# A graph network's edge loop: groups of edges taken in pairs, in place of one by one

## The chip, the core and the metric

The kernel runs on one core of one Trainium2 chip. The metric is the device time of one execution in microseconds (us). The core has five engines that run beside each other, each with its own queue, in order: PE (TensorE, matmuls and transposes; its weight loads are shown as PEld), DVE (VectorE), ACT (ScalarE), POOL (GpSimd) and SP (SyncE, here only a DMA queue). ACT and POOL issue DMAs too.

## The reference, cut to what matters

A graph network over 12500 nodes of 64 values and 200000 edges, sorted by destination:

```
nodes = x[edges]                               # rows of source and destination, side by side: 128 values
gates = ssp(edge_state @ We1 + be1) @ We2 + be2
gates = gates * (1 - sigmoid(5 * (distance - 3.5)))
h = ssp(nodes @ Wn1 + bn1) @ Wn2 + bn2
message_sum = zeros_like(x).at[destination].add(h * gates)
new = x + ssp(message_sum @ Ws1 + bs1) @ Ws2 + bs2
out = layernorm(x + new)
```

`ssp` is softplus less log 2. So each edge needs two small networks (one over its own 64 values, one over its two nodes), a product, and an addition into its destination's row; each node then needs one more small network and a layernorm.

## The kernel before, in words

**Tiling.** The edges are cut into 391 groups of 512, each of four slots of 128 edges. All is float32, but for biases, which come as three bfloat16 pieces. A step of the main loop (line 697) does the first layer of group i+1 and the second layer of group i.

**Where the node rows come from.** The source rows of a slot are gathered from memory by an indirect DMA that POOL issues (`gather`, line 248, the DMA on line 258), 14 groups ahead (`AHEAD`), into one of 19 buffers `xg`. Such a buffer is free when the scatter of the group 19 before has read it. Two other ways take some slots off POOL. 26 slots are fetched row by row by DMAs on ACT's queue, nine rows in each step (`read_rows` and `fetch`, lines 265 and 276: three after the copy of the transposes, three after the exp, three after the log; the row numbers come from memory into registers, line 272). 23 slots are copied by DVE, eight columns in a step, out of a transposed x that lies in SBUF (`columns`, line 319). So 1514 gathers remain of 1564 slots. The destinations of a sorted group fall into two windows of 42 rows; their first layer is worked out ahead for all nodes into a table in DRAM, and `load` (line 300) brings a group's windows of that table (`wns`) and its edge values (`eT`) by SP.

**A step, engine by engine.** The code writes out the order by hand (`manual_schedule`), and each engine follows it:

- PE: `transposes` of group i+1 (four), `layer1_bias`, `layer2_bias` of group i, `scatter` of group i-2 (messages times one-hots, into windows), `layer1_edge`, `layer1_node`, and `layer2` of group i (two matmuls for the gates, four for the nodes, which need the softplus of group i).
- ACT: `xcopy` (the transposes out of PSUM), `exps` over 768 columns, `logs`, and between them the nine row DMAs.
- DVE: `window` (scattered sums added to `sums` in SBUF), `hcut` (second layer of the nodes times the distance factor), `message` (times the gates), `softplus` (an SBUF and a PSUM operand), `onehot` of group i+3, and the column copies.

PSUM holds two `z` tiles of two banks, two `gh` tiles and two `tx` tiles. In the second layer the edges lie on the partitions, so gates, nodes and messages come out with one edge per partition.

**Nodes.** 25 blocks of up to 512 nodes are finished as soon as no later group can add to them; their parts (`node_block`, line 455) are spread over the steps that follow, with PE's parts after `layer2`. The last twelve steps scatter one group back in place of two (`CLOSE`). The two last groups and the last block are written out after the loop (from line 749).

**Ahead of the loop** stands the preparation: table rows by PE, ACT and DVE, and the first 14 groups' gathers.

## Time and profile before

| | us |
|---|---|
| median of 3 runs | 1936.83 (1936.46 to 1937.05) |
| the profiled execution's own time | 1936.46 |
| its span, first to last instruction | 1934.7 |
| first transposes of the loop | at 79.5 |
| first gather issued, last gather issued | at 3.3, at 1906.3 |
| PE, DVE, ACT, POOL busy | 1776.3, 1299.2, 965.0, 1441.5 |

In the profile's lines a line number is that of the kernel's code, `out<-in` names tiles, `x` and a number is a count. ACTq and SPq are the queues of ACT and SP issuing DMAs, which do not count as busy time. In a wait, the engine and line on the left stood idle until the one on the right was done; the numbers are the total in us, how often, and the longest. "issue" is time in which an engine waited for nothing that the profile shows. PE's ends are modelled: matmuls overlap, so the starts tell more than the lengths.

### The profile page before, as it was taken

What the parts mean: (1) busy time and instruction counts of PE and PEld (TensorE: products, weight loads), DVE (VectorE), ACT (ScalarE), POOL (GpSimd) and SP (SyncE); (2) the same over time, 40 slices, a digit from 0 to 9 for tenths busy, and PEclk for the clock granted to TensorE, in tenths of its full rate; (3) what the DMA queues carried; (4) which work ended last, traced back from release to release, by engine and by line L of the source; (5) the groups of instructions that cost most, each with busy time, mean ns of one, the idle gap of its engine ahead of it and who ended that gap; (6) DMA issues with size and microseconds to landing.
All of it is one profiled execution on the core that took longest, in us unless ns stands there. A gap on an engine that the chain in (4) does not pass through costs nothing.

```text
span 1934.7 us, 48239 instructions
## 1 busy us (share of the span) xinstructions
PE 1776.3 (92%) x11419; PEld 1458.4 (75%) x11419; DVE 1299.2 (67%) x5743; ACT 965.0 (50%) x1318; POOL 1441.5 (75%) x1518
## 2 busy tenths in 40 slices
PE   4899999999999989899999998999999999999997
PEld 3787877877787777777777777777787777777775
DVE  4467776777776666666667666676677667677765
ACT  1355555555555545544445554554455555555553
POOL 7777777777777777777777777777777777777773
PEclk9999999999999999999999999999899999999998
DMA  9632222223232222222232222222232222233221
GB/s 245 230 80 66 71 73 65 72 66 73 66 74 67 64 70 64 69 65 70 64 69 67 68 69 67 70 69 67 64 75 68 69 70 70 69 73 72 70 66 25
DMA packets 146498, 147.57 MB, mean 76 GB/s; under 512 B 46735, under 2 KB 93371, under 8 KB 146082
## 3 DMA queue, kind: packets, MB, share of 16 engines
q1 hardware_dynamic: 89578, 92.27, 16.5%
q0 software_dynamic: 48448, 49.71, 13.4%
q10 hardware_dynamic: 8184, 2.44, 0.6%
q8 instruction: 97, 1.59, 0.3%
q14 instruction: 191, 1.56, 0.3%
HBM read 134.61 MB, written 9.63 MB: 75 GB/s over the span
## 4 chain that ended last, share of the span: by engine, by line
PE 43%; ACTq 19%; issue 10%; DVE 8%; ACT 8%; DMA 7%; DVEq 2%; POOL 2%; SPq 1%; POOLq 0%
ACTq L284 16%; PE z L380 9%; PE gh L419 6%; PE z L436 6%; PE tx L356 5%; PE z L373 4%; ACT xT L363 4%; PE gh L414 4%; DMA xg<-in_x,src_i 3%; ACTq L272 3%; ACT u L394 2%; POOL xg L258 2%; DVE h L428 2%; PE gh L407 2%; PE z L368 2%
## 5 line engine op out<-in xcount | busy, mean ns | idle before, releaser
L258 POOL DMA_INDIRECT xg<-in_x,src_i x1514 | 1441.3, 952 | 465.5 <-issue 332.9
L394 ACT ACTIVATE u<-z 128x768 f32<-128x768 f32 x392 | 317.4, 810 | 693.3 <-PE z L380 591.8
L453 DVE TENSOR_TENSOR sums<-sums,z 64x42 f32 x778 | 153.0, 197 | 498.2 <-ACT u L394 457.5
L380 PE MATMUL z<-xT,wns 106*128 106x256 f32 x1564 | 422.7, 393 | 10.5 <-ACT xT L363 10.1
L397 ACT ACTIVATE u<-u,one 128x768 f32<-128x768 f32 x392 | 366.1, 934 | 67.3 <-ACT u L394 62.4
L419 PE MATMUL gh<-consts,s 128*128 128x64 f32 x3128 | 397.6, 270 | 0.0
L419 PEld LDWEIGHTS gh<-consts,s 128*128 128x128 f32 x3128 | 387.0, 195 | 0.1
L402 DVE SCALAR_TENSOR_TENSOR s<-u,z 128x768 f32<-128x768 f32 x392 | 369.0, 941 | 12.2 <-ACT u L397 10.4
L380 PEld LDWEIGHTS z<-xT,wns 106*128 106x128 f32 x1564 | 297.2, 195 | 76.8 <-ACT xT L363 31.6
L356 PE MATMUL tx<-consts,xg 128*106 128x128 f32 x1538 | 239.5, 276 | 94.2 <-DVE h L428 22.0
L436 PEld LDWEIGHTS z<-xg,msg 128*128 128x128 f32 x1556 | 205.2, 192 | 125.2 <-issue 122.6
L363 ACT COPY xT<-tx 106x512 f32<-106x512 f32 x391 | 228.2, 584 | 128.1 <-PE tx L356 119.2
L332 DVE COPY column<-xh 128x1 f32 x2944 | 266.3, 147 | 25.6 <-issue 24.6
L436 PE MATMUL z<-xg,msg 128*128 128x84 f32 x1556 | 265.4, 293 | 0.4
L414 PEld LDWEIGHTS gh<-consts,s 128*128 128x128 f32 x1564 | 240.5, 196 | 29.7 <-DVE s L402 8.8
L356 PEld LDWEIGHTS tx<-consts,xg 128*106 128x106 f32 x1538 | 172.1, 140 | 111.6 <-issue 57.2
L373 PE MATMUL z<-eT,consts 128*128 128x256 f32 x782 | 254.0, 407 | 0.0
L414 PE MATMUL gh<-consts,s 128*128 128x128 f32 x1564 | 245.8, 280 | 3.9 <-DVE s L402 3.6
L428 DVE TENSOR_TENSOR h<-gh,cut 128x256 f32<-128x256 f32 x391 | 165.9, 424 | 27.9 <-PE gh L419 15.1
L432 DVE TENSOR_TENSOR msg<-gh,h 128x256 f32<-128x256 f32 x391 | 165.9, 424 | 13.4
L407 PE MATMUL gh<-row,ones 3*128 3x512 bf16 x391 | 147.3, 377 | 0.0
L342 DVE TENSOR_TENSOR xg<-consts,rel 128x168 f32<-128x168 f32 x391 | 128.3, 328 | 0.0
(102 smaller groups left out, 725.8 us busy)
## 6 DMA issues: line engine op xcount, KB each, us to landing
xr<-in_x ACTq DMA_DIRECT2D x3328, 0.2 KB
eT<-in_eT SPq DMA_DIRECT2D x195, 256.0 KB
xg<-in_x,src_i POOLq DMA_INDIRECT x1514
wns<-table SPq DMA_DIRECT2D x782, 21.0 KB
table<-tb SPq DMA_DIRECT2D x14, 448.0 KB
sums<-in_xT SPq DMA_DIRECT2D x7, 455.0 KB
y<-in_x SPq DMA_DIRECT2D x24, 128.0 KB
out<-y SPq DMA_DIRECT2D x24, 128.0 KB
```

What stands on the lines that cost most here:

```text
L258: note(("gather", g), nc.gpsimd.indirect_dma_start(out=xg[:, k, :D], out_offset=None, in_=x, in_offset=bass.IndirectOffsetOnAxis(ap=src_i[ ...
L284: ins = queues[queue].dma_start(row_tiles[n, "in"][r : r + 1, :D].bitcast(U8), x_bytes[:, bass.ds(row_at[queue].pop(0), 4 * D)])
L356: ins = nc.tensor.transpose(tx[:, k, :], xgs[g][:, k, :DW], ident)
L363: note(("xcopy", g), nc.scalar.copy(xT, xTs[g]))
L373: nc.tensor.matmul(zs[g][:, 0, :HE], we1.rearrange("a h d -> a (h d)"), eTs[g], start=False, stop=True, skip_group_check=True)
L380: nc.tensor.matmul(zn, wns[:, g % REST, h, :], xTs[g][:, h], start=True, stop=not chosen, skip_group_check=True)
L394: nc.scalar.activation(us[g][:, part], z_of(g)[:, part], AF.Exp)
L397: nc.scalar.activation(us[g][:, part], us[g][:, part], AF.Ln, bias=one)
L402: nc.vector.scalar_tensor_tensor(ss[g].rearrange("p i t e -> p (i t e)")[:, part], us[g][:, part], BIG, z_of(g)[:, part], OP.min, OP.max)
L414: nc.tensor.matmul(v[:, 0, t], ss[g][:, 0, t, :], we2, start=False, stop=False, skip_group_check=True)
L419: nc.tensor.matmul(ghs[g][:, 1, 2 * t + h, :], ss[g][:, 1 + h, t, :], wn2, start=False, stop=h == 1 and t == 1, skip_group_check=True)
L436: ins = nc.tensor.matmul(sc, msgs[g][:, 2 * t : 2 * t + 2, :].rearrange("p h f -> p (h f)"), xgs[g][:, 2 * t : 2 * t + 2, D:DW], start=t = ...
```

## The change

Groups 0 to 371 are taken in 186 pairs. A pair p (groups 2p and 2p+1) is worked like this:

- **First layer, in two halves.** `pair_edge` does bias and edge matmul for both groups at once (512 columns), `pair_node` the nodes of the first group into the same z tile; `pair_exps`, `pair_logs` and `pair_softplus` take these 1024 columns in one instruction each, then the second group's 512 columns in another.
- **Second layer, transposed.** `pair_gates` (one matmul over 512 columns) and `pair_hidden` (two over 512 columns, for the two halves of the output's partitions) leave the values on the partitions and the edges along the columns. So the biases become one value per partition: ACT adds the gates' (`pair_bias`, a new instruction over 512 columns), DVE adds the nodes' and multiplies by the gates in one instruction (`pair_products`). The bias matmul of the second layer goes. PE transposes the product back (`pair_turn`, four), and DVE multiplies by the distance factor (`pair_weigh`), which gives the messages. `hcut` and `message` go.
- **Scatter** of the pair before stands between `pair_hidden` and `pair_turn`; its windows are added after the second exp.
- **Other work.** Per pair: 18 row DMAs on ACT in six threes, sixteen column copies on DVE in two blocks of eight, two groups' loads and gathers. Column slots are used two groups later after their copies. The table rows are loaded two groups further ahead (`LOADS` 7, nine buffers), and wait for the scatter of 15 groups before in place of 9. The signs that choose between the two halves of the transposed x come in 23 small transfers, one per slot, in place of one transfer and one scaling ahead of the loop; each slot has a mask instruction for it.
- The remaining groups (from the 373rd on) go one by one as before, scattering one group back, with one-hots one group earlier and one buffer for the exps in place of two.

The number of gathers, of row DMAs and of column copies stays. The diff, cut to its core:

```diff
-LOADS = 5
+LOADS = 7
-CLOSE = 12
+PAIRS = 186
...
-        if (g - 3 - COLUMNS_FROM + 1) * COLUMNS >= (len(slots) + 1) * P:
+        if (g - 5 - COLUMNS_FROM + 1) * COLUMNS >= (len(slots) + 1) * P:
...
-        old = ("scatter", g - LOADS - 4)
+        old = ("scatter", g - LOADS - 8)
...
+            side_tiles[slot] = pool.tile([P, P], I32, name="side", bufs=1)
+            nc.sync.dma_start(side_tiles[slot], a["sides"][n : n + P].partition_broadcast(P))
...
+            mask = pool.tile([P, P], F32, name="mask", bufs=1)
+            nc.vector.tensor_scalar(mask, side_tiles[slot], sign, border, OP.mult, OP.is_ge)
...
+            nc.vector.tensor_mul(chosen_columns[slot], mask, column_tiles[slot])
...
-            us[g] = work.tile([P, 3 * HE], F32, name="u")
+            us[g] = work.tile([P, 4 * HE], F32, name="u0", bufs=1)[:, : 3 * HE]
...
+    def pair_edge(p):
+        z1s[p] = z_tile()
+        nc.tensor.matmul(z1s[p][:, 0], be3.rearrange("q h d -> q (h d)"), ones3, start=True, stop=False,
+                         skip_group_check=True)
+        nc.tensor.matmul(z1s[p][:, 0], we1.rearrange("a h d -> a (h d)"), eT2s[p], start=False, stop=True,
+                         skip_group_check=True)
+
+    def pair_node(p, j):
+        z = (z2s if j else z1s)[p]
+        for h in range(2):
+            node_half(2 * p + j, h, z[:, 1, h * HE : (h + 1) * HE])
+
+    def pair_z(p, j):
+        return z2s[p][:, 1] if j else z1s[p].rearrange("p b e -> p (b e)")
+
+    def pair_exps(p, j):
+        u2s[p, j] = work.tile([P, (2 if j else 4) * HE], F32, name=f"u{j}", bufs=1)
+        nc.scalar.activation(u2s[p, j], pair_z(p, j), AF.Exp)
+
+    def pair_logs(p, j):
+        nc.scalar.activation(u2s[p, j], u2s[p, j], AF.Ln, bias=one)
+
+    def pair_softplus(p, j):
+        if j == 0:
+            s2s[p] = work.tile([P, 6 * HE], F32, name="s2")
+        nc.vector.scalar_tensor_tensor(s2s[p][:, slice(4 * HE, 6 * HE) if j else slice(0, 4 * HE)], u2s[p, j], BIG,
+                                       pair_z(p, j), OP.min, OP.max)
+
+    def pair_gates(p):
+        gates2[p] = gh_tile()
+        nc.tensor.matmul(gates2[p], we2.rearrange("a h d -> a (h d)"), s2s[p][:, :NB], start=True, stop=True,
+                         skip_group_check=True)
+
+    def pair_hidden(p):
+        hidden2[p] = gh_tile()
+        nodes = s2s[p][:, NB:].rearrange("p (j h e) -> p h j e", j=2, h=2)
+        for h in range(2):
+            nc.tensor.matmul(hidden2[p][h * D : (h + 1) * D].rearrange("p (j e) -> p j e", j=2), wn2, nodes[:, h],
+                             start=True, stop=True, skip_group_check=True)
+
+    def pair_bias(p):
+        turned2[p] = work.tile([P, NB], F32, name="mT")
+        nc.scalar.activation(turned2[p], gates2[p], AF.Identity, bias=sides2[:, 0:1])
+
+    def pair_products(p):
+        nc.vector.scalar_tensor_tensor(turned2[p], hidden2[p], sides2[:, 1:2], turned2[p], OP.add, OP.mult)
+
+    def pair_turn(p):
+        for t in range(K):
+            part = slice(t * P, (t + 1) * P)
+            nc.tensor.transpose(hidden2[p][:, part], turned2[p][:, part], ident)
+
+    def pair_weigh(p):
+        msg2s[p] = work.tile([P, 2, K, D], F32, name="msg2")
+        nc.vector.tensor_mul(msg2s[p].rearrange("p j k d -> p (j k) d"), hidden2[p].rearrange("p (k d) -> p k d", d=D),
+                             cut[:, 2 * p : 2 * p + 2, :].rearrange("p j k -> p (j k)").to_broadcast([P, 2 * K, D]))
+
+    def pair_scatter(p, sc):
+        for j in range(2):
+            msgs[2 * p + j] = msg2s[p][:, j]
+            scatter(2 * p + j, sc[:, j * 2 * W : (j + 1) * 2 * W])
+
+    def pair_windows(p):
+        _, at = nc.values_load_multi_w_load_instructions(
+            base_i[0:1, 4 * p : 4 * p + 4], engines=[DVE], min_val=0, max_val=N - 1,
+            skip_runtime_bounds_check_because="they were clamped to these bounds")
+        for j in range(2):
+            window_at[2 * p + j] = at[2 * j : 2 * j + 2]
+            window(2 * p + j)
...
-                    nc.vector.tensor_scalar(sides, sides_i, sign, None, OP.mult)
...
+            for p in range(-1, PAIRS):
+                i, m, single = 2 * p, 2 * p + 2, p == PAIRS - 1
+                now = [parts.pop(i, []), parts.pop(i + 1, [])]
+                for j in range(2):
+                    at(load, i + LOADS + 1 + j)
+                if 0 <= p < XH_PARTS:
+                    part = slice(half_n * p // XH_PARTS, half_n * (p + 1) // XH_PARTS)
+                    nc.sync.dma_start(xh[:, part], a["xh"][:, part])
+                for j in range(2):
+                    if p >= 0:
+                        at(gather, i + AHEAD + j)
+                transposes(m, ("load", m), ("gather", m), ("onehot", m))
+                xcopy(m)
+                read_rows(i, 1, ROWS[1])
+                fetch(i, 1, 3)
+                if single:
+                    layer1_bias(m)
+                    layer1_edge(m)
+                else:
+                    pair_edge(p + 1)
+                if p >= 0:
+                    pair_gates(p)
+                    pair_bias(p)
+                if p >= 1:
+                    pair_weigh(p - 1)
+                fetch(i, 1, 3)
+                if single:
+                    layer1_node(m)
+                    exps(m)
+                else:
+                    pair_node(p + 1, 0)
+                    pair_exps(p + 1, 0)
+                fetch(i, 1, 3)
+                transposes(m + 1, ("load", m + 1), ("gather", m + 1), ("onehot", m + 1))
+                for j in range(2):
+                    at(onehot, i + 4 + j)
+                for j in range(2):
+                    columns(i + j, finish)
+                if p >= 0:
+                    pair_hidden(p)
+                for part in now[0] + now[1]:
+                    if part.tensor:
+                        part.tensor(tx_tile())
+                if p >= 0:
+                    pair_products(p)
+                if single:
+                    logs(m)
+                    xcopy(m + 1)
+                    layer1_bias(m + 1)
+                    layer1_edge(m + 1)
+                else:
+                    pair_logs(p + 1, 0)
+                    xcopy(m + 1)
+                    z2s[p + 1] = z_tile()
+                read_rows(i + 1, 1, ROWS[1])
+                fetch(i + 1, 1, 3)
+                if p >= 1:
+                    pair_scatter(p - 1, zs[m + 1][:, 1, HE:] if single else z2s[p + 1][:, 0])
+                if p >= 0:
+                    pair_turn(p)
+                if single:
+                    layer1_node(m + 1)
+                    exps(m + 1)
+                    fetch(i + 1, 1, 3)
+                    logs(m + 1)
+                    softplus(m)
+                else:
+                    pair_node(p + 1, 1)
+                    pair_exps(p + 1, 1)
+                    fetch(i + 1, 1, 3)
+                    pair_logs(p + 1, 1)
+                    pair_softplus(p + 1, 0)
+                fetch(i + 1, 1, 3)
+                for part in now[0]:
+                    part.others()
+                if p >= 1:
+                    pair_windows(p - 1)
+                if single:
+                    softplus(m + 1)
+                else:
+                    pair_softplus(p + 1, 1)
+                for part in now[1]:
+                    part.others()
+                plan(i)
+            for i in range(2 * PAIRS + 1, last - 1):
...
+                if i == open_at + 1:
+                    pair_weigh(PAIRS - 1)
+                    layer2_bias(open_at)
+                    layer2(open_at)
+                    hcut(open_at)
+                    message(open_at)
+                layer1_bias(i + 1)
+                if i == open_at + 1:
+                    pair_scatter(PAIRS - 1, zs[i + 1][:, 1, HE:])
+                    layer1_edge(i + 1)
+                    layer1_node(i + 1)
+                    layer2_bias(i)
+                    scatter(i - 1, zs[i + 1][:, 1, HE + 4 * W : HE + 6 * W])
+                else:
+                    layer2_bias(i)
+                    scatter(i - 1, zs[i + 1][:, 1, HE : HE + 2 * W])
+                    layer1_edge(i + 1)
+                    layer1_node(i + 1)
+                exps(i + 1)
...
```

## The prediction

> **What bounds the kernel now.** I read the page's shares first: PE is busy for 92% of the span, POOL for 75%. Busy time alone would name PE, so the second view is POOL's own: the gather's line and its waits.
>
> ```profile
> PE 1776.3 (92%) x11419; PEld 1458.4 (75%) x11419; DVE 1299.2 (67%) x5743; ACT 965.0 (50%) x1318; POOL 1441.5 (75%) x1518
> ```
>
> ```profile
> L258 POOL DMA_INDIRECT xg<-in_x,src_i x1514: 941/947/2392, 3.3 to 1906.3; - x190
> ```
>
> ```profile
> POOL xg L258 <- issue: 332.9, 1091, 0.3
> POOL xg L258 <- DMA xg<-in_x,src_i: 40.3, 129, 1.0
> ```
>
> 1514 gathers have a median of 0.947 us (the three numbers are shortest, median, longest), and before each POOL stands 0.3 us whatever is named; only two such gaps are longer, the longest 1.0. So gathers follow each other every 1.25 us without a break: from 3.3 to 1906.30 + 0.95 = 1907.25 us that is 1903.9 us, 1.257 each, and 4.87 us per group. POOL is never held up; the 75% are 0.947/1.25.
>
> Third, the stages: busy time by stretch, and the waits of PE in two stretches.
>
> ```profile
> 100.00:300.00 200.00, 197.89 (x1333) 161.08 (x1331) 138.99 (x628) 109.65 (x142) 151.34 (x160) 1.00 0.29 71
> 600.00:800.00 200.00, 181.80 (x1179) 148.96 (x1178) 133.30 (x604) 99.31 (x134) 151.19 (x161) 0.98 0.28 66
> ```
>
> ```profile
> PE z L380 <- ACT xT L363: 3.8, 10, 0.6
> ...
> PE tx L356 <- DVE h L428: 21.0, 29, 1.3
> PE tx L356 <- DVE msg L432: 18.3, 15, 1.6
> PE tx L356 <- DVE sums L453: 13.5, 24, 1.3
> PE tx L356 <- DMA xg<-in_x,src_i: 11.5, 12, 1.5
> ```
>
> Columns of the first: stretch, length, busy time (records) of PE, PEld, DVE, ACT, POOL, then clock and DMA. POOL is the same in both; PE is full early and not later. A step has 28 matmul records (4+1+1+4+2+4+4+8), so 1333 are 47.6 steps: 4.20 us each. In the waits, the first line is from 100 to 560 us, where no transposes wait at all; the others are from 600 to 1900, where the first transposes of a step wait. Those DVE lines name work long done; the gather's landing is what is left. So the gathers start 71 us ahead (group 0's fourth ends at 7.21 + 0.95 = 8.2, its transposes begin at 79.5), PE gains 0.67 us a group, has caught up near 600, and then POOL sets the pace. At the end group 390 is transposed 2.3 us after the last gather, and 25.1 us of tail follow.
>
> ```profile
> 1906.30 0.95 POOL L258 DMA_INDIRECT xg<-in_x,src_i  x1 [0.30 <-issue]
> ...
> 1909.58 0.60 PE L356 MATMUL tx<-consts,xg 128*106 128x128 f32 x4
> ```
>
> Fourth, one early step on ACT, where nothing waits for gathers:
>
> ```profile
> 300.96 0.94 ACT L397 ACTIVATE u<-u,one 128x768 f32<-128x768 f32 x1 [0.16 <-ACT u L394]
> 301.04 0.85 ACTq L284 DMA_DIRECT2D xr<-in_x  x3
> 301.93 0.59 ACT L363 COPY xT<-tx 106x512 f32<-106x512 f32 x1
> 302.89 1.09 ACTq L284 DMA_DIRECT2D xr<-in_x  x3
> 304.08 0.81 ACT L394 ACTIVATE u<-z 128x768 f32<-128x768 f32 x1 [1.56 <-PE z L380]
> 304.16 0.85 ACTq L284 DMA_DIRECT2D xr<-in_x  x3
> 305.05 0.94 ACT L397 ACTIVATE u<-u,one 128x768 f32<-128x768 f32 x1 [0.16 <-ACT u L394]
> ```
>
> ACT's queue, 50% busy by its share, is full here: exp to log 0.97, log to copy 0.97, copy to exp 2.15 (a register load of 0.8 and three row loads), 4.09 in all. PE's starts in the same step also add up to 4.09: transposes 0.54, two biases 0.12 and 0.30, scatter 0.51, edges 0.47, nodes 0.87, second layer 0.44 and 0.84. Both would carry 4.09; POOL gives 4.87.
>
> **The change part by part.** The sum is made against the profiled execution, 1936.46 us: 3.3 before the first gather, 1903.9 of gathers, 27.5 after them, 1.8 around the span. It is the lowest of the three runs, 0.4 below their median.
>
> *POOL.* Row slots (26) and column slots (23) keep their number, so 1514 gathers remain: 0. They need the xg buffer of 19 groups before, freed by that group's scatter. Laid out with the rows above, the pairs' transposes begin at 79.5, 85.6 (no second layer comes before) and 94.7 (9.1 later), and scatter(0), 7 us on in that pair, ends near 101.7; gather 19 comes at 103.9. Cover 2.2 us, growing by over half a us per pair: 0, at worst a few us once if the start slips.
>
> *PE per pair.* 8 transposes 1.08, bias over 512 columns 0.30 (the 512-wide bf16 row), edges and gates 512 wide twice the 256-wide 0.47 at most, 0.90 each, nodes 1.74, hidden two 512-wide 1.80 (0.9 if its two halves, on different output partitions, run together; no row shows it, I take 1.80), scatter 1.02, four transposes back 0.54: 8.3, against 8.2 for two steps.
>
> *DVE per pair.* Softplus 512 and 768 wide take 0.68 and 0.94, so 1024 takes 1.20; second softplus 0.68; products 0.68; weigh 0.69 (0.42 at 256, and 0.26 per 256); windows 0.80; one-hots 0.66; columns 2 x 0.63 and 0.6 for the second register load: 6.6, against 6.3. Waits it adds: products stand behind hidden and, in DVE's order, behind the copies (these end about 8.5 us after the pair's first log, hidden at 8.8), and the turn on PE, with the second nodes behind it, waits for products; windows wait for the second exp, and second softplus, weigh, one-hots and copies queue behind them, with about 0.7 us to spare before hidden ends. If that cover goes, the excess lands on the second nodes.
>
> *ACT per pair*, along its queue, where it is tightest. Log over 1024: 0.51, 0.72, 0.93 at 256, 512, 768, so 1.15, less the 0.09 by which an independent instruction starts before its neighbour's end (a 0.51 log at 1913.18, the next exp at 1913.60); copy 0.59; nodes and the way to the next exp 1.25 (302.52 to 303.70, and 0.07); exp to log with three loads 0.97; log to copy 0.97; copy, register load and three loads 2.09; the new bias with three loads 1.03 (its 0.58 lies under them); exp over 1024 1.05 and 0.04. Sum 9.05. The second register load and three loads lie under log and copy. So a pair takes 9.05 where nothing disturbs it, against 8.18 for two steps: slower free, but below POOL's 2 x 4.87 = 9.74. Node blocks add 0.8 of ACT per block (log pair 0.45, root 0.33), 24 blocks, 0.1 per pair; their PE and DVE parts, mostly covered, as much; slow-clock stretches 0.1 (the late clock is 0.97, 3% of PE's 8.3 is 0.25, and its slack of 0.8 takes over half). I take 9.35, between 9.05 and 9.6; the upper end carries twice the 0.25 by which before's free steps exceed 4.09 on average (from 100 to 560 us, 106 second-layer biases are recorded, 4.34 each).
>
> *Does it still catch up?* 94.7 + 184 pairs + 18 groups x 4.09 must be at most 1909.6, less 3 for the change-over (step 373 carries a second layer more, 1.3, and waits for its message, 1.7): the limit is 9.44 per pair. At 9.35 PE reaches the gathers before the end.
>
> *SP's queue, single steps, tail.* Loads for two groups are issued per pair, for three pairs later (28 us), and wait for a scatter two pairs back; 23 small side transfers stand among them. Waits for table rows, 8.4 us in all after 600 us, lie in the gathers' waits anyway: 0, and if the loads came late, such waits again. The single steps have one buffer for exps in place of two: softplus ends at 303.02, the next exp comes at 304.08, so 0. The last 330 instructions of PE and 420 of DVE are the same in both, so the tail stays; its clock is 0.51 from 1917 on, and a shift of that costs or saves 1 to 2 us.
>
> *Start.* The scaling of sides goes. A gather beside it (45.16, 1.84 instead of 0.95) loses 0.9: -0.9. All stretched gathers before 90 us together lose 7; they bound the gain.
>
> Sum: 1936.46 - 0.9 = about 1936.
>
> **Rules weighed.** Row: a gather beside eight column copies (303.12, copies from 303.18) takes 0.97, and the median of all is 6 ns over the shortest. I price sixteen copies in one block at 0, and if each of 186 blocks cost 0.02 more, at 4 us. The Trainium skill, SBUF — State Buffer, section SBUF: two separate sides, says that an fp32 copy within SBUF locks GpSimd out of descriptor writing; by it up to 16 x 0.147 = 2.4 us per pair would be lost, 437 us in all. The scaling of sides agrees with it, one-column copies do not.
>
> Row: PE waited 1.46 us before 1007.46, and from 1009.0 to 1012.4 the clock was 0.55. The change gathers PE's waits into one of about 1.3 us per pair, which may call such stretches oftener; one costs up to 1.7 us, and the slack above 9.05 makes it good in three pairs, so I price it at 0.1. The Trainium skill, TensorE: Matmul & The Clock Gate, section Why this matters for your kernels, asks only for gaps under about 3 us; by it the price is 0. The row contradicts that.
>
> **Rivals.**
> 1. *Slower: the pair's own pace sets the end.* Place: ACT's queue from log to log, through copy and second nodes. For: 9.35 has only 0.1 to spare, and 9.6 lies in its bounds. Against: double register loads, the main excess there, are covered in the pair. From 9.44 on it decides, 18.4 us per 0.1: at 9.6, 1966; at 9.8, 2003. Chance 0.39.
> 2. *Faster: fewer stretched gathers.* At most -7 and -2 of tail: 1928 to 1933. For: traffic and a 1.77 us DVE instruction leave the start. Against: the other casts there stay. 0.07.
> 3. *The change doesn't tell* (forecast): gathers set the end. 0.54.
>
> **How the numbers follow.** 0.2% (3.9 us) is about what a measurement here can tell from no change: 1932.9 to 1940.7. The forecast's own range is 1933 to 1940. Two in ten are left out: 0.06 below 1932, 0.14 of the slower case above 1966.
>
> **What would show it.** Right: gathers every 1.25 us to about 1907, PE waiting at the transposes of a pair's second group late in the run, ACT's chain 9.1 long early on. Wrong: POOL gaps over 0.3 us late in the run (buffers not freed), or the transposes never waiting for gathers, or copies stretching gathers.

## The result, and the profile after

| | before | after |
|---|---|---|
| median | 1936.64 us (1936.19 to 1937.05, 4 runs) | 1945.54 us (1944.63 to 1951.97, 4 runs) |
| the profiled execution, its span | 1936.46, 1934.7 | 1944.63, 1942.8 |
| first transposes of the loop | 79.5 | 82.0 |
| last gather done | 1907.2 | 1912.3 |
| last group's transposes behind it | 2.3 | 5.2 |

The ratio is 1.0053, with a 95% interval of 1.0031 to 1.0075: slower by some 9 us. I had forecast 1936.0. Of the 8.1 us between the two spans, 5.1 are there when the last gather is done, and 3.0 come behind it (from its end to the end of the span it is 30.5 us instead of 27.5).

From the page of the changed kernel, PE's share and the gathers, and from POOL's waits the line of the ordinary gap and the line that is new (total us, how often, longest):

```profile
PE 1669.8 (86%) x7887; PEld 1022.7 (53%) x7887; DVE 1306.3 (67%) x5396; ACT 1069.6 (55%) x1504; POOL 1442.5 (74%) x1518
...
L257 POOL DMA_INDIRECT xg<-in_x,src_i x1514 | 1442.3, 953 | 469.6 <-issue 320.7
```

```profile
POOL xg L257 <- issue: 320.7, 1051, 0.3
...
POOL xg L257 <- DVE mT L506: 6.2, 4, 5.1
```

PE has 107 us less to do, and it bought nothing. POOL has the same 1514 gathers at the same 0.95 us, but one wait of 5.1 us among them that the kernel before did not have.

The stages by busy time (PE, PEld, DVE, ACT, POOL, then clock, DMA share, GB/s):

```profile
100.00:300.00 200.00, 177.75 (x818) 104.61 (x816) 128.34 (x525) 114.12 (x154) 147.49 (x156) 0.98 0.31 79
600.00:800.00 200.00, 177.30 (x811) 104.48 (x811) 137.17 (x587) 113.44 (x156) 151.46 (x160) 0.98 0.28 68
1500.00:1700.00 200.00, 168.09 (x801) 98.35 (x800) 138.86 (x592) 114.12 (x164) 151.49 (x160) 1.00 0.28 69
```

POOL is level at 151 from 600 us on, as before; in the first stretch it has 156 gathers where the kernel before had 160. PE is no longer full early (178 of 200, before 198).

PE's waits from 100 to 560 us (two lines, all that the view has), then from 1400 to 1830 us:

```profile
PE z L381 <- ACT xT L366: 36.9, 48, 1.4
PE gh L511 <- DVE mT L506: 14.3, 21, 2.6
...
PE tx L359 <- DMA xg<-in_x,src_i: 26.4, 22, 1.8
PE tx L359 <- DMA wns<-table: 12.0, 13, 1.9
```

Early, PE waits within the pair: for ACT's copy of the second transposes, and for DVE's products. Late, the transposes wait for the gathers (13 of the waits are put down to the table rows, `wns`, which land about then). So the order of things is the forecast's: the pair's own chain sets the pace first, the gathers later. The lag of a group's transposes behind its last gather says when: 57.7 us at group 20, 3.1 at group 260 (transposes at 1285.2), and then about 2 (1.9 in the median, never under 1.5) up to group 374. It ends otherwise than before:

```profile
1911.38 0.95 POOL L257 DMA_INDIRECT xg<-in_x,src_i  x1 [0.30 <-issue]
...
1917.56 0.60 PE L359 MATMUL tx<-consts,xg 128*106 128x128 f32 x4
```

### Where the first 5 us come from

The start, from the timelines (start, length, then what ended the idle time before it). L651 in the kernel before and L727 in the changed one are the matmuls of the table ahead of the loop, L356 and L359 the transposes; L745 are the new matmuls that make the biases of the transposed second layer, L440 is the scatter. First PE in the kernel before, up to the transposes of group 2; then the changed kernel: PE ahead of the loop, PE in its first steps, and POOL, where the first line is the 77th gather in the kernel before (L258) and the last the 77th in the changed one:

```profile
35.08 12.32 PE L651 MATMUL z<-consts,sums 65*128 65x128 f32 x56 [10.98 <-DVE tb L654]
48.32 24.26 PE L651 MATMUL z<-consts,sums 65*128 65x128 f32 x112 [0.93 <-DVE tb L654]
79.50 1.07 PE L356 MATMUL tx<-consts,xg 128*106 128x128 f32 x4 [6.92 <-DMA wns<-table]
...
90.19 1.06 PE L356 MATMUL tx<-consts,xg 128*106 128x128 f32 x4
```

```profile
33.82 6.34 PE L727 MATMUL z<-consts,sums 65*128 65x128 f32 x28 [9.15 <-DVE tb L730]
44.38 0.21 PE L745 MATMUL gh<-ones,rows 3*128 3x1 bf16 x2 [4.21 <-DVE rows L742]
44.52 30.71 PE L727 MATMUL z<-consts,sums 65*128 65x128 f32 x140
```

```profile
82.00 1.07 PE L359 MATMUL tx<-consts,xg 128*106 128x128 f32 x4 [6.78 <-DMA wns<-table]
...
90.08 2.07 PE L381 MATMUL z<-xT,wns 106*128 106x256 f32 x4 [1.91 <-ACT xT L366]
91.95 1.06 PE L359 MATMUL tx<-consts,xg 128*106 128x128 f32 x4
...
101.32 0.60 PE L359 MATMUL tx<-consts,xg 128*106 128x128 f32 x4
...
106.60 1.12 PE L440 MATMUL z<-xg,msg 128*128 128x84 f32 x8
```

```profile
103.87 0.94 POOL L258 DMA_INDIRECT xg<-in_x,src_i  x1 [0.30 <-issue]
...
101.45 0.95 POOL L257 DMA_INDIRECT xg<-in_x,src_i  x1 [0.31 <-issue]
107.55 0.95 POOL L257 DMA_INDIRECT xg<-in_x,src_i  x1 [5.15 <-DVE mT L506]
```

Two tiny matmuls (0.21 us) stand in PE's order in the middle of the table's matmuls and wait 4.21 us for a DVE copy; 140 table matmuls queue behind them. In the kernel before PE's table work ran from 35.08 to 72.58 us with one gap of 0.93; here it ends at 75.2, and the loop starts 2.5 us later. Then the first pair is slow: PE's matmuls take up to twice as long (four transposes 1.06 us, 0.60 later), and PE waits 1.91 us for the copy. Half the clock is the likely reason. The clock's view does not show it here (1.00 from 80 to 95 us), but in late_fewer, one of the runs below, the same transposes (at 88.14 there) take 1.06 too, and the clock is 0.71 from 85 to 90 us and 0.61 from 90 to 95. The kernel before starts as slowly. So the first scatter comes at 106.60, and the gather that needs its buffer, the 77th (76 in the expectations, which count from 0), starts at 107.55, where it could have started at 102.7. (The profile puts this wait down to DVE's products, L506, which end at about the same time. The buffer is the one that group 0's scatter reads, the first four of the eight matmuls at 106.60.) These 4.8 us are never won back, since the gathers run at their own pace from there to the end: 1804.8 us from that one's start to the last one's end, where the kernel before took 1803.4. The sum for POOL is 4.8 of waiting and 1.4 of slightly slower gathers, less 1.2 that it is ahead before the wait: 5.1 with the unrounded numbers.

### Where the last 3 us come from

The passage from pairs to single steps, PE's timeline:

```profile
1837.82 0.60 PE L359 MATMUL tx<-consts,xg 128*106 128x128 f32 x4
...
1841.44 1.12 PE L440 MATMUL z<-xg,msg 128*128 128x84 f32 x8 [1.01 <-DVE msg L515]
...
1845.98 0.38 PE L359 MATMUL tx<-consts,xg 128*106 128x128 f32 x2
...
1848.35 0.68 PE L440 MATMUL z<-xg,msg 128*128 128x84 f32 x4 [1.34 <-DVE msg L436]
...
1852.82 0.74 PE L579 MATMUL tx<-consts,l_s 128*128 128x128 f32 x4 [0.97 <-DVE l_s L571]
1853.39 0.60 PE L359 MATMUL tx<-consts,xg 128*106 128x128 f32 x4
```

From the transposes of group 374 to those of 376 it is 15.6 us, where two free single steps would take 8.2: PE does the second layer of group 372 and the scatter of the last pair beside the work of two single steps, and waits three times, twice for messages and once for a node block. The lag goes from 2.1 (group 374) to 8.9 (376). The fourteen groups that remain take 4.58 us each; the lag falls to 5.2, and there the gathers end. The kernel before has no such passage; from group 374 on its lag lies between 1.8 and 4.7, and it ends at 2.3.

### The profile page after: what moved, and what is told of

Read it like the earlier page. It is cut to its first block, busy times and chain, and to the rows that moved or that the text cites. A ratio compares the mean times of both kernels' runs of the same rounds, so it can differ in the third digit from the quotient of the medians.

```text
span 1942.8 us, 41448 instructions
## 1 busy us (share of the span) xinstructions
PE 1669.8 (86%) x7887; PEld 1022.7 (53%) x7887; DVE 1306.3 (67%) x5396; ACT 1069.6 (55%) x1504; POOL 1442.5 (74%) x1518
## 4 chain that ended last, share of the span: by engine, by line
PE 27%; ACTq 24%; ACT 18%; issue 12%; DMA 8%; DVE 6%; POOL 3%; DVEq 2%; SPq 0%; POOLq 0%
ACTq L283 21%; PE z L381 11%; ACT u L478 6%; ACT u L481 6%; DMA xg<-in_x,src_i 6%; ACT xT L366 4%; POOL xg L257 3%; ACTq L271 2%; PE z L440 2%; PE gh L498 2%; PE tx L359 2%; PE z L465 2%; DVE column L334 2%; PE z L727 2%; PE gh L511 2%
## 5 line engine op out<-in xcount | busy, mean ns | idle before, releaser
L478 ACT ACTIVATE u<-z 128x1024 f32<-128x1024 f32 x372 | 301.6, 811 | 336.0 <-PE z L381 256.4
L486 DVE SCALAR_TENSOR_TENSOR s<-u,z 128x1024 f32<-128x1024 f32 x372 | 354.5, 953 | 177.4 <-ACT u L481 173.5
L481 ACT ACTIVATE u<-u,one 128x1024 f32<-128x1024 f32 x372 | 347.9, 935 | 79.8 <-ACT u L478 74.0
L359 PE MATMUL tx<-consts,xg 128*106 128x128 f32 x1538 | 240.4, 276 | 66.9 <-DMA xg<-in_x,src_i 30.9
L503 ACT ACTIVATE mT<-gh,sides 128x512 f32<-128x512 f32 x186 | 127.8, 687 | 274.5 <-PE z L381 203.9
L440 PEld LDWEIGHTS z<-xg,msg 128*128 128x128 f32 x1556 | 190.8, 191 | 126.9 <-issue 116.1
L359 PEld LDWEIGHTS tx<-consts,xg 128*106 128x106 f32 x1538 | 182.0, 133 | 127.4 <-issue 62.1
L440 PE MATMUL z<-xg,msg 128*128 128x84 f32 x1556 | 215.6, 280 | 4.2 <-DVE msg L436 2.3
L465 PE MATMUL z<-eT,consts 128*128 128x512 f32 x372 | 216.3, 664 | 0.0
L498 PE MATMUL gh<-s,consts 128*64 128x512 f32 x744 | 200.7, 618 | 0.0
L506 DVE SCALAR_TENSOR_TENSOR mT<-gh,sides,mT 128x512 f32<-128x512 f32 x186 | 139.5, 750 | 84.8 <-PE gh L498 80.3
L491 PE MATMUL gh<-s,consts 128*128 128x512 f32 x372 | 195.5, 608 | 0.0
L511 PE MATMUL gh<-consts,mT 128*128 128x128 f32 x744 | 120.3, 284 | 43.3 <-DVE mT L506 42.0
L515 DVE TENSOR_TENSOR msg<-gh,cut 128x512 f32<-128x512 f32 x186 | 125.7, 676 | 0.0
```

Source lines behind the costliest of these rows:

```text
L359: ins = nc.tensor.transpose(tx[:, k, :], xgs[g][:, k, :DW], ident)
L440: ins = nc.tensor.matmul(sc, msgs[g][:, 2 * t : 2 * t + 2, :].rearrange("p h f -> p (h f)"), xgs[g][:, 2 * t : 2 * t + 2, D:DW], start=t = ...
L465: nc.tensor.matmul(z1s[p][:, 0], we1.rearrange("a h d -> a (h d)"), eT2s[p], start=False, stop=True, skip_group_check=True)
L478: nc.scalar.activation(u2s[p, j], pair_z(p, j), AF.Exp)
L481: nc.scalar.activation(u2s[p, j], u2s[p, j], AF.Ln, bias=one)
L486: nc.vector.scalar_tensor_tensor(s2s[p][:, slice(4 * HE, 6 * HE) if j else slice(0, 4 * HE)], u2s[p, j], BIG, pair_z(p, j), OP.min, OP.max)
```

## The experiments

The first set ran on one chip beside the kernel before, which took 1933.81 us there (1932.69 to 1936.17, 13 runs); its gathers are a little quicker (every 1.249 us in the median, 1.251 in the two profiles above). Ratios are to the kernel before on the same chip; the changed kernel's is 1.0053.

### The new matmuls behind the table's (late_sides)

```diff
                     for k in range(2):
                         nc.vector.tensor_copy(be3[:, k, :], rows[:, 0, :])
                         nc.vector.tensor_copy(rows2[:, :, k, :], rows[:, 1:3, :])
-                    ps = gh_tile()
-                    for q in range(2):
-                        nc.tensor.matmul(ps[:, q : q + 1], rows2[:, q]..., ones3[:, :1], start=True, stop=True)
-                    nc.vector.tensor_copy(sides2, ps[:, :2])
...
+            ps = gh_tile()          # after the loop over the table's parts
+            for q in range(2):
+                nc.tensor.matmul(ps[:, q : q + 1], rows2[:, q]..., ones3[:, :1], start=True, stop=True)
+            nc.vector.tensor_copy(sides2, ps[:, :2])
```

> The changed kernel, with the two matmuls that make sides2 behind all table matmuls instead of among them. Theory: in PE's order they wait 4.21 us for a DVE copy while the table's matmuls queue behind, so the table, the loads, the first transposes (82.0) and the first pair's scatter come late, and gather 76 stands 5.15 us for its buffer. Then first transposes at 77.7 to 78.6, the gap before gather 76 falls from 5.15 to between 0.8 and 1.8, time 3.4 to 4.4 below the changed kernel, 1941.1 to 1942.1 against its 1945.5. Rival (SP's queue and the table's writes set the first transposes, not PE): first transposes stay at 82, gap 5.15, 1945.5.

Measured: 1941.38 us, ratio 1.0039 (1.0026 to 1.0052). From its timeline, PE ahead of the loop and at its first transposes, and the gather after the wait:

```profile
34.50 36.68 PE L727 MATMUL z<-consts,sums 65*128 65x128 f32 x168 [9.85 <-DVE tb L730]
71.11 0.21 PE L756 MATMUL gh<-ones,rows 3*128 3x1 bf16 x2
```

```profile
104.06 0.94 POOL L257 DMA_INDIRECT xg<-in_x,src_i  x1 [1.61 <-DVE mT L506]
```

The place is shown: the table's matmuls run without a break, the first transposes come at 78.1 in place of 82.0, and the wait falls from 5.15 to 1.61, all inside the theory's bounds. The time gained less than expected (by its ratio 2.7 us less than the changed kernel, with intervals that overlap; the pair of runs with 170 pairs, below, shows the gain on one chip). More was lost at the passage: there the lag went from 2.0 to 12.2, and 8.5 were left at the end. The windows over the passage show the difference, first for this kernel, then for the changed one (the number before the last two is the granted clock):

```profile
1840.00:1850.00 10.00, 8.67 (x40) 6.58 (x37) 8.67 (x42) 3.19 (x5) 7.56 (x9) 0.68 0.22 58
1850.00:1860.00 10.00, 9.89 (x56) 8.22 (x55) 4.62 (x22) 4.46 (x7) 7.56 (x9) 0.81 0.23 61
```

```profile
1840.00:1850.00 10.00, 7.65 (x50) 6.03 (x50) 5.88 (x23) 3.40 (x6) 7.56 (x9) 1.00 0.15 32
```

After the same two waits of the passage (here 1.01 and 1.33 us) PE ran at about half clock for some 10 us (the transposes of group 376, at 1847.95, take 1.06), and the lag at the end is 3.3 us more.

### One gather buffer more (more_buffers)

```diff
-BEHIND = 5
+BEHIND = 6
...
-                    tb = prep.tile([P, m, 2 * D], F32, name="tb", bufs=6)
+                    tb = prep.tile([P, m, 2 * D], F32, name="tb", bufs=5)
```

(and one `y2`, `l_s` and `zb` tile each in place of two, to make room)

> The changed kernel with 20 xg buffers in place of 19 (room for it: five table tiles in place of six, one y2, l_s and zb tile in place of two). Theory: the early gap is a wait for a buffer that the first pair's scatter frees; with one buffer more the wait moves to gather 80, 5.0 us later by the gathers' pace, so 5.15 becomes 0.3 or at most 0.6, with the first transposes still at 82: 4.6 to 4.9 less, 1940.7 to 1940.9. Rival (the early gap is made good later, or is not what the end is made of): 1945.5.

Measured: 1941.21 us, ratio 1.0035 (1.0023 to 1.0047). POOL's waits from 60 to 140 us begin with this line, and none of the others is over 0.3 us either:

```profile
POOL xg L257 <- issue: 17.4, 57, 0.3
```

The gap is gone, as expected, by another means than in the run before. So the 5 us are a buffer that comes free late, and not, say, the gathers' own transfers. The first transposes came at 79.7, two us earlier than I had said, which stays unexplained. The lag after the passage was 12.5 and at the end 9.0, with a clock of 0.59 from 1840 to 1850 us: again the passage ate part of the gain. What is left over the kernel before, 7.4 us, is about what the last transposes lag more (9.0 against 2.3 in the kernel before's profile), so the start and the passage together account for the loss. No run takes both away.

### Fewer pairs (fewer_pairs), and both edits (late_fewer)

```diff
-PAIRS = 186
+PAIRS = 170
```

> The changed kernel with 170 pairs in place of 186, so that 32 more groups go one by one. Theory: passing from pairs to single steps costs PE 7.3 us (the transposes stand 1.6 us behind the gathers before and 8.9 after it), which single steps win back at about 0.35 us a group, and 14 groups are too few; with 46 groups the last transposes follow the last gather by 2.3 us as before, not 5.2: 2.9 less, 1942.6. The early gap of 5.15 stays. Rival (the lag belongs to the changed single steps with their one exp buffer, not to the passage): the lag stays at 5 or more, 1945.5 or longer.

> Both of the edits above together. Theory: the two losses are independent, in time one after the other: 6.3 to 7.3 below the changed kernel, 1938.2 to 1939.2, and within 0.2% of the kernel before (1936.6). Rival (pairs cost elsewhere too, by traffic or clock): 1941 or more.

Measured: 1949.81 us, ratio 1.0076 (1.0063 to 1.0089), and with the later matmuls 1941.85 us, ratio 1.0036 (1.0023 to 1.0049). The two differ in the place of the new matmuls alone and ran on one chip, and their intervals lie apart: the later matmuls are worth 8.0 us here. In their profiles the last gather ends 4.3 us sooner with them (1907.2, before 1911.5), POOL's longest wait for a buffer falls from 5.4 to 2.5, and the lag at the end is 0.8 less; the medians differ by more than that, and why stays open. My theory's time is refuted for both: passing earlier made it slower, not faster, and late_fewer met the time of its rival (1941 or more). The lags tell which part of it fell (us behind the last gather, at groups 340, 350, 360, 390):

| | 340 | 350 | 360 | 390 |
|---|---|---|---|---|
| before | 2.2 | 2.9 | 1.9 | 2.3 |
| changed, 186 pairs | 1.6 | 2.8 | 2.0 | 5.2 |
| 170 pairs | 1.5 | 16.6 | 12.9 | 9.7 |
| 170 pairs, matmuls later | 1.4 | 16.0 | 12.5 | 8.9 |

The passage is where the lag arises: moved from group 373 to 341, the jump moved with it, and the rival (the single steps make the lag) falls, since single steps shrink it from 16.6 to 9.7, though both of its figures came (a lag of 5 or more, and 1945.5 or longer). What fell is that the jump has one size, and that 46 groups win it back. At group 341 the row DMAs still run (they end near step 370), and the passage issues those of two groups in one step. ACT's queue there:

```profile
1686.72 5.05 ACTq L283 DMA_DIRECT2D xr<-in_x  x12
1691.87 0.81 ACT L398 ACTIVATE u<-z 128x768 f32<-128x768 f32 x1 [5.20 <-issue]
...
1699.02 0.30 ACT L595 ACTIVATE rstd<-var,eps 128x4 f32<-128x4 f32 x1 [5.24 <-DVE var L591]
```

and PE in the same stretch:

```profile
1695.36 0.68 PE L440 MATMUL z<-xg,msg 128*128 128x84 f32 x4 [2.40 <-DVE msg L436]
...
1700.08 2.08 PE L381 MATMUL z<-xT,wns 106*128 106x256 f32 x4 [3.57 <-ACT xT L366]
```

Twelve row DMAs hold ACT for 5 us, the next exp starts after them, DVE's windows and messages wait for it, and then ACT itself stands 5.2 us before a node block's root with the copy behind it. And single steps win back only 0.17 us a group (16.6 to 9.7 over 40 groups), not 0.35, up to group 370, where the row DMAs end (12.9 there), hardly otherwise than behind it.

### Gathers taken off the kernel before (sp_rows, sp_rows_again, sp_rows_3)

```diff
-ROWS = (0, 9)
+ROWS = (6, 9)
...
                 at(load, i + LOADS)
+                read_rows(i, 0, ROWS[0])
+                fetch(i, 0, ROWS[0])
```

> As for sp_rows. On a chip that takes 1935 us for the kernel before. Theory (gathers set the end): 22.6 us less, ratio 0.988. Rival (PE or ACT sets it): within 4 us. On a chip like those of the last sets: 1% slower than the kernel before, as there.

Measured (sp_rows_3): 1914.06 us beside 1934.71 for the kernel before, ratio 0.9896 (0.9879 to 0.9912). This is 1% less than the kernel before, and it changes nothing but who loads 18 slots. Its gathers from the page, then its end from the timeline:

```profile
L258 POOL DMA_INDIRECT xg<-in_x,src_i x1496 | 1422.4, 951 | 458.9 <-issue 336.2
```

```profile
1880.86 0.95 POOL L258 DMA_INDIRECT xg<-in_x,src_i  x1 [0.30 <-DMA xg<-in_x,src_i]
1884.91 0.60 PE L356 MATMUL tx<-consts,xg 128*106 128x128 f32 x4
```

1496 gathers, done at 1881.8; the last transposes 3.1 us behind. 18 x 1.249 = 22.5 us were to go, and 20.6 went. So gathers set the end of the kernel before, and PE, at 92% of the span, was not what held it.

### Sets on chips that stood still

The same kernel, and four more, also fell on chips where the kernel before took 2600 to 2670 us. There engines stand for up to 5 us at a time in the loop of either kernel, and nothing about the 9 us can be read from them. A stretch of sp_rows shows it (timeline; "remote" is the profile's word for another core or an unknown queue):

```profile
1007.16 0.42 DVE L428 TENSOR_TENSOR h<-gh,cut 128x256 f32<-128x256 f32 x1 [3.06 <-remote]
1007.25 0.58 ACT L363 COPY xT<-tx 106x512 f32<-106x512 f32 x1 [1.90 <-remote]
...
1007.56 0.94 POOL L258 DMA_INDIRECT xg<-in_x,src_i  x1 [1.49 <-remote]
```

The transposes that the copy needs had begun at 1003.59 and were long done; DVE, ACT and POOL set off again together. Instructions of ACT, DVE and POOL take as long as ever (a gather 0.944 us in the median, an exp 0.81), but PE's matmuls take longer: the mean granted clock of the kernel before is 0.82 to 0.86 there, where it is 0.97 to 0.98 on the others. What holds the engines stayed open. One thing the profiles add: from 300 to 1900 us the waits put down to "remote" sum to some 250 us in after_again and 380 in sp_rows, to 6 in before_free and to none in after_free, so they go where a quarter of the gathers goes.

The edits: the changed kernel unaltered (after_again, after_same_chip); 192 pairs, `PAIRS = 192` (more_pairs, late_change); and both kernels with slot 0 of each group from the 15th on loaded by SP, always the same 128 rows of x, so that the rows these edges ask for are left out:

```diff
+            if k == 0 and g >= AHEAD:
+                note(("gather", g), nc.sync.dma_start(xg[:, k, :D], x[:P, :]))
+                continue
             note(("gather", g), nc.gpsimd.indirect_dma_start(
```

The expectations, in the order after_again, after_same_chip, more_pairs, late_change, before_free, after_free, before_unbound, after_unbound, after_unbound_2, after_unbound_3, sp_rows, sp_rows_again (most kernels stand twice or more, since they were run again on another chip):

> The changed kernel unaltered, beside the kernel before on one chip, as the measure for the others of this set. 8 to 10 us above the kernel before.

> The changed kernel unaltered once more, on another chip than the last set's, whose engines stood still for microseconds at a time and which took 2600 us for the kernel before. 8 to 10 us above the kernel before.

> The changed kernel with 192 pairs in place of 186: the passage to single steps comes 12 groups later. Theory: the passage itself costs 7 us of the transposes' lag behind the gathers, and single steps win some of it back; with 12 steps fewer to do so the last transposes follow the last gather by 8 to 9 us in place of 5.2, and the time is 3 to 4 us longer than the changed kernel's. Rival (the single steps, not the passage, make the lag): with fewer single steps the lag at the end is smaller than 5.2, and the time at most the changed kernel's.

> The changed kernel with 192 pairs in place of 186: the passage to single steps comes 12 groups later. Theory: the passage itself costs 7 us of the transposes' lag behind the gathers, and single steps win some of it back; with 12 steps fewer to do so the last transposes follow the last gather by 8 to 9 us in place of 5.2, and the time is 3 to 4 us longer than the changed kernel's. Rival (the single steps, not the passage, make the lag): with fewer single steps the lag at the end is smaller than 5.2, and the time at most the changed kernel's.

> The kernel before, with slot 0 of every group from the 15th on loaded by one plain transfer on SP's queue (the first 128 rows of x) in place of a gather: the output is wrong by that, and POOL has 377 gathers fewer, so that it should no longer set the pace. Theory: the free pace of 4.34 us a group runs to the end: 79.5 + 390 x 4.34 + 25 = 1797 span, 1785 to 1815. Rival (gathers were not what both kernels end by): 1900 or more.

> The changed kernel with the same slot 0 loaded by SP (output wrong by that). Theory: a pair's own pace of 9.26 us runs to the end: 82 + 186 x 9.26 + 7 for the passage + 18 x 4.3 + 25 = 1914 span, 1895 to 1925, so some 110 us slower than the kernel before under the same cut, where with gathers the two differ by 9. Rival (pairs are as fast in themselves, and the 9 us are only the start and the end): within 20 us of the kernel before under the same cut.

> The kernel before, with slot 0 of every group from the 15th on loaded by one plain transfer on SP's queue (the first 128 rows of x) in place of a gather, so that the output is not the reference's; POOL has 377 gathers fewer and should no longer set the pace. Theory: the free pace of 4.34 us a group runs to the end: 79.5 + 390 x 4.34 + 25 = 1797 span, 1785 to 1815. Rival (gathers were not what both kernels end by): 1900 or more.

> The changed kernel with the same slot 0 loaded by SP (output not the reference's by that). Theory: a pair's own pace of 9.26 us runs to the end: 82 + 186 x 9.26 + 7 for the passage + 18 x 4.3 + 25 = 1914 span, 1895 to 1925, so some 110 us slower than the kernel before under the same cut, where with gathers the two differ by 9. Rival (pairs are as fast in themselves, and the 9 us are only the start and the end): within 20 us of the kernel before under the same cut.

> As for after_unbound, on another chip. If that chip takes some 1935 us for the kernel before. Theory: a pair's own pace of 9.26 us runs to the end, 1895 to 1925, no more than 2% below the changed kernel, though POOL has a quarter of its gathers less. Rival (gathers alone set the pace of the changed kernel and its pairs are free to go faster): 1800 or less. If the chip is like those of the last sets, 2200 to 2225 as there.

> As for after_unbound, on another chip. On a chip that takes 1935 us for the kernel before. Theory: a pair's own pace of 9.26 us runs to the end, 1895 to 1925, no more than 2% below the changed kernel, though POOL has a quarter of its gathers less. Rival (gathers alone hold the changed kernel back, its pairs could go at two free steps' pace): 1800 or less.

> The kernel before with six rows a step fetched by SP's queue too (its code for that is there with a count of zero): 18 more slots come row by row, so 1496 gathers in place of 1514. Theory (gathers at 1.257 us set the end, PE has over half a us a group to spare): 18 x 1.257 = 22.6 us less, 1911 to 1916, a ratio of 0.988. SP's queue then has some 4.6 us of issues in a step of 4.81; if that overflows, table rows and edge values come late and the gain shrinks. Rival (the 8 us of the change show that PE or ACT sets the end, not the gathers): within 4 us of the kernel before.

> As for sp_rows, on another chip: the kernel before with six rows a step fetched by SP's queue too, 1496 gathers in place of 1514. Theory (gathers at 1.257 us set the end): 22.6 us less than the kernel before, ratio 0.988; if SP's queue overflows the gain shrinks. Rival (PE or ACT sets the end): within 4 us of the kernel before. If the chip is like those of the last sets (the kernel before at 2600), neither is tested.

| run | kernel before, same chip | this | ratio |
|---|---|---|---|
| after_again | 2616.59 | 2570.63 | 0.9869 (0.9822 to 0.9916) |
| after_same_chip | 2621.80 | 2572.19 | 0.9816 (0.9773 to 0.9859) |
| more_pairs | 2616.59 | 2566.95 | 0.9852 (0.9805 to 0.9900) |
| late_change | 2621.80 | 2564.97 | 0.9778 (0.9731 to 0.9825) |
| before_free, before_unbound | 2616.59, 2621.80 | 2080.79, 2085.61 | 0.7989, 0.7959 |
| after_free, after_unbound | 2616.59, 2621.80 | 2224.80, 2212.29 | 0.8542, 0.8442 |
| after_unbound_2, after_unbound_3 | 2607.85, 2611.82 | 2219.08, 2217.90 | 0.8503, 0.8491 |
| sp_rows, sp_rows_again | 2618.76, 2666.86 | 2654.72, 2691.05 | 1.0125 (1.0074 to 1.0176), 1.0100 (1.0035 to 1.0165) |

None of these is a test of the theories as they were put: in after_again PE stands 6.8 us in all before transposes, so gathers set no pace there. What they do say is small. With a quarter of the gathers gone, the changed kernel is 6 to 7% slower than the kernel before with the same gathers gone (2224.80 to 2080.79, 2212.29 to 2085.61), the direction that the pair's longer chain gives; its size is not that of an undisturbed chip. All of these times lie far above their theories (1797 and 1914): in before_free no transposes wait for gathers and the clock is 0.99, yet a step takes 4.91 us (groups 100 to 300), not the free 4.34. Why is open. And the signs of two results turn round: on such a chip the changed kernel is the faster one by 1.3 to 1.8%, and loading more rows by SP costs 1%. The late passage with 192 pairs was not tried on an undisturbed chip, nor were the two kernels freed of a quarter of their gathers.

## Why the prediction was wrong, point by point

**Right: what bounds the kernel.** Gathers at their own pace, POOL held up only once, PE not the bound at 92%. PE lost 107 us of work and the time rose; 18 gathers fewer took 20.6 us off.

**Right: the pair's own pace, and that it still catches up.** I had taken 9.35 us a pair, between 9.05 and 9.6. From group 20 to group 260 it is (1285.2 - 173.8) / 120 = 9.26. The chain is the one that I laid out on ACT's queue; one pair of it, from log to log, in the changed kernel's timeline:

```profile
299.80 1.15 ACT L481 ACTIVATE u<-u,one 128x1024 f32<-128x1024 f32 x1
...
300.85 0.57 ACT L366 COPY xT<-tx 106x512 f32<-106x512 f32 x1
...
302.80 0.60 ACT L478 ACTIVATE u<-z 128x512 f32<-128x512 f32 x1 [1.38 <-PE z L381]
...
303.77 0.72 ACT L481 ACTIVATE u<-u,one 128x512 f32<-128x512 f32 x1 [0.38 <-ACT u L478]
...
304.73 0.59 ACT L366 COPY xT<-tx 106x512 f32<-106x512 f32 x1 [0.24 <-issue]
...
306.87 0.69 ACT L503 ACTIVATE mT<-gh,sides 128x512 f32<-128x512 f32 x1 [1.55 <-PE z L381]
...
307.91 1.02 ACT L478 ACTIVATE u<-z 128x1024 f32<-128x1024 f32 x1 [0.36 <-issue]
...
308.97 1.15 ACT L481 ACTIVATE u<-u,one 128x1024 f32<-128x1024 f32 x1
```

The starts are 9.17 apart, where my terms add up to 9.05: log to copy 1.05, copy to exp 1.95 (I had 1.84), exp to log 0.97, log to copy 0.96, copy to bias 2.14 (2.09), bias to exp 1.04, exp to log 1.06. The bias itself is 0.69 (0.58 estimated), under the row DMAs as I had it. Rival 1 needed 9.44 and did not come: the time lies in the range that was given to it, but from another cause. On PE a term came out smaller: I took 1.80 for the two 512-wide matmuls of `pair_hidden`, and in the changed kernel the scatter starts 1.01 us after them (105.59 to 106.60), while one such matmul of `pair_gates` fills 0.96 (103.13 to 104.09). So the two halves took the time of one; PE was not what held the kernel, and nothing came of it.

**Wrong: "*Start*", the sum of "pairs' transposes begin at 79.5, 85.6 ... and 94.7", and with it "Cover 2.2 us ... 0, at worst a few us once if the start slips".** This is the step that failed first. The transposes begin at 82.0, 91.95 and 101.32, the freed gather at 107.55 where I had the scatter's end at 101.7. Of these 5.85 us, 2.5 are the two new matmuls in PE's order ahead of the loop (late_sides puts their whole price at 3.9, from 82.0 to 78.1), which I had not costed at all: I listed what the change takes out of the start (the scaling of the signs) and not what it puts in. 3.85 are the first pair, 9.95 long in place of 6.1: I had laid it out with the lengths of later steps, and its matmuls take up to twice as long (four transposes 1.06 us, later ones 0.60). The kernel before showed this price: there the first two steps take 10.7 us (79.50 to 90.19, with transposes of 1.07), in place of 8.2. 0.3 are the second pair's, and the scatter came 0.8 sooner in its pair than I had it. I had named the term, the buffer and the place, and had put the price at 0 with a cover of 2.2; with a cover that thin, its failure belonged into the likeliest case.

**Wrong: the change-over, "less 3 for the change-over", made good by single steps.** It cost 7.4 us in two steps in place of 3, and the single steps gain about a quarter of a us each on the gathers (8.9 to 5.2 over 14), so that the last transposes lag 2.9 us more than in the kernel before. I had used it only for the limit of 9.44 a pair, took it as recovered, and left what follows the last gather as it was ("so the tail stays"): 27.5 us, where 30.5 were measured.

**Not shown, and small: the -0.9 for the scaling of the signs.** In this profile the gathers ahead of the wait stand 1.2 us earlier than before (76th at 101.45 in place of 102.62). But the 76th comes at 101.64 in sp_rows_3, which keeps the scaling, and at 101.81 in fewer_pairs, which lacks it: from one profile to the next it differs by as much. And all stretched gathers before 90 us lose 5.5 us, not the 7 of the prediction: in the kernel before the 76th starts 99.3 us after the first, and 75 steps of 1.251 are 93.8.

**Right: copies do not stretch gathers.** With the column copies in blocks of sixteen, the 1514 gathers have a median of 0.947 us over a shortest of 0.940 (0.947 and 0.941 in the kernel before), and from 600 to 800 us POOL is busy for 151.46 us (160 records), where the kernel before has 151.19 (161). Here the row was the better guide: the Trainium skill, SBUF — State Buffer, section SBUF: two separate sides, would have had fp32 copies lock GpSimd out.

**The clock.** I had priced half-clock stretches at 0.1 us a pair, from a row where a PE wait of 1.46 us was followed by one. The pairs' pace left room for that. The place where it hurt was another: in late_sides waits of 1.01 and 1.33 us at the passage were followed by some 10 us at about half clock (0.68 and 0.81 over two stretches of 10 us), while the changed kernel's own profile has the same waits (1.01 and 1.34) and a clock of 1.00. The Trainium skill, TensorE: Matmul & The Clock Gate, section Why this matters for your kernels, warns only of gaps above about 3 us; the rows of late_sides show half clock after shorter ones, those of the changed kernel's profile do not, and what decides between them no run here shows. That this is what spreads the runs of the pair kernels (1937.87 to 1944.55 in late_sides, 1937.01 to 1947.48 in more_buffers, where the kernel before keeps within 3.5 us) is likely, but only one profile of each was taken.

## What to carry to other kernels

When one engine issues without a break from start to end, the time is its first start, its work and the tail behind it: work taken off other engines is worth nothing by itself, and each wait that it suffers once, at the start or at a change of stage, is paid in full. So cost the few places where the steady state begins and ends as carefully as the loop, each instruction in the queue where it is put; here a 0.2 us matmul in the wrong place cost more than 107 us of saved matmuls gave. And a change that helps must touch the bound: moving 18 of 1514 gathers to SP's queue gave 1%.

## What was not expected of the hardware

- The same code took 2600 to 2670 us on some chips and 1934 to 1937 on others, with ACT, DVE and POOL instructions as long as ever, a granted clock of 0.82 to 0.86 in place of 0.97 to 0.98 in the kernel before, and engines that stood still together; the order of the two kernels, and the worth of SP's row DMAs, were the opposite there.
- A half-clock stretch of 10 us followed PE waits of 1.0 and 1.3 us in two profiles of the passage (0.68 in late_sides, 0.59 in more_buffers, from 1840 to 1850 us) and not in a third with the same waits.
- Twelve row DMAs issued in a row, with the register load among them, held ACT's queue for 5.05 us; three take 0.85 to 1.16 in the changed kernel.
- Two 512-wide float32 matmuls on different halves of the output's partitions took 1.01 us together, one over all 128 partitions 0.96.
